# Source lookups of a graph attention layer: one PSUM tile per half chunk becomes one fixed PSUM tile used in two quarters

## The chip, the cores and the metric

The kernel runs on one core of a Trainium2 chip. The metric is device time in microseconds (us). The engines are TensorE (PE in the profile; its weight loads are PEld), VectorE (DVE), ScalarE (ACT), GpSimd (POOL) and SyncE (SP, which here only issues DMAs). An instruction of one engine that needs the result of another waits for a semaphore count, and each engine runs its own list of instructions strictly in order.

## The reference, cut to what matters

There are 6250 nodes with 128 features and 100,000 edges, sorted by destination. Two graph convolutions come first, then an attention layer over the same edges, each followed by a residual sum and a layer norm. The part that matters here is the attention layer:

```python
z = h @ fc_w.T
rh = r_h @ fc_r_w.T
zs = z[src]
zd = z[dst]
e = zs @ aw[0] + zd @ aw[1] + rh @ aw[2]
e = jnp.where(e >= 0, e, NEG_SLOPE * e)
m = jax.ops.segment_max(e, dst, num_segments=N)
ex = jnp.exp(e - m[dst])
alpha = ex / jax.ops.segment_sum(ex, dst, num_segments=N)[dst]
agg = jax.ops.segment_sum(alpha[:, None] * (zs + rh), dst, num_segments=N)
out = jax.nn.relu(agg + z @ loop_w)
```

`zs @ aw[0]` is one number per node, fetched for each edge by the node that the edge starts from. That fetch, 100,000 lookups in a table of 6250 numbers, is what the change is about.

## The kernel before, in words

Edges are cut into 49 chunks of 2048 (`NC`, `CC`), and nodes into 49 blocks of 128 (`NB`). The program has stages one after the other: preparation and sorting, first convolution, second convolution (with the dot products of edge features beside it), and the attention stage, which is the last and holds everything that follows.

In the attention stage two strands run together. The main loop goes over the chunks: `shares` places the attention shares of a chunk (L1254 to L1264), `pick` gathers the rows of source nodes by matmuls with a 0/1 mask and by indirect DMAs (L532, L537, L541), `scatter` sums them by destination (L578), `edge_part` does the same with the edge features (L1280 to L1304), and `Pieces` finishes blocks of nodes as they are complete. The other strand, `scores`, works out the attention shares ahead of the loop, in eight batches of chunks (2, 5, then 7 chunks each): `ends` looks up the destination's number, `starts` the source's, and `softmax` turns a batch into shares. The first main-loop chunk of a batch can't begin before that batch's softmax is done. `scores` is a generator; `deal` takes so many of its steps at fixed points of the main loop, and each `yield` in it ends a step.

`starts(c)` handles a chunk in two halves of 1024 edges, so there are 98 half chunks in all. For each half, a row of source numbers modulo 128 is loaded and broadcast to all partitions (`rk`, L1105), and turned into a 0/1 matrix by VectorE (L1138). VectorE also makes `ohb`, which marks the block of each edge (L1140). TensorE then multiplies, for each of the half's 8 groups of 128 edges, the 0/1 matrix with the table of 49 blocks, three times because the table is split into three bf16 parts (L1145): 24 matmuls into a PSUM tile `k` of 128x392 float32. VectorE multiplies the tile by `ohb` into `sel` (L1148) and sums over the blocks (L1149), which leaves one number per edge in `asr`. The pool `ps_k` has one buffer, one PSUM bank; the pools of the stage take all eight banks. `sel` has one buffer too.

The order in which instructions stand on each engine isn't the program's text order. A scheduler orders them when the program is built, by priorities that follow the text (and the steps of `deal`) and by when it reckons each instruction is ready. The instructions of `starts` are so mixed with those of the main loop. The order is fixed once built, and the semaphore waits are put in then, after a tracking of which instruction touches which tile.

Of the kernel before, what the change touches and what calls it, by code (L numbers as in the profile page):

```python
# [9 lines left out]
F32 = mybir.dt.float32  # L10
# [9 lines left out]
P = 128  # L20
# [7 lines left out]
NL = CC // P  # L28
# [10 lines left out]
def gnn_kernel(ctx, tc, x, src, dst, ea, ew, W1, b1, W2, b2, fcw, fcrw, attn, loopw, out):  # L39
# [11 lines left out]
    nc = tc.nc  # L51
# [3 lines left out]
    NB = -(-N // P)  # L55
# [155 lines left out]
    adp = keep.tile([P, 2, 3, NB + 1], BF16, name="adp")  # L211
# [386 lines left out]
    with tc.tile_pool(name="prep", bufs=1) as prep, tc.tile_pool(name="ps_p", bufs=3, space=PSUM) as ps_mm, \  # L598
# [113 lines left out]
        ps = ps_mm.tile([P, 4, D], F32, name="mm")  # L712
# [134 lines left out]
    def steps_to(c):  # L847

        b = next(b for b, (c0, n) in enumerate(sorts) if c < c0 + n)
        return 2 * sum(sorts[b]) + b + 1  # L850

    with tc.tile_pool(name="xs0", bufs=1) as xp, tc.tile_pool(name="ps_d", bufs=3, space=PSUM) as ps_mm, \
# [8 lines left out]
        with tc.high_priority():  # L861
            for c0 in range(0, NC, 7):
# [4 lines left out]
                for c in range(c0, c0 + n):  # L867
                    m = ms[:, c - c0]
                    ps = ps_w.tile([3, WC], F32, name="win")
# [11 lines left out]
            ps = ps_w.tile([P, NB], F32, name="win")  # L881
# [9 lines left out]
    with tc.tile_pool(name="conv", bufs=2) as wp, tc.tile_pool(name="hp", bufs=2) as hp, \  # L891
# [18 lines left out]
        start, total = done[0], steps_to(NC - 1)  # L910
# [169 lines left out]
    with tc.tile_pool(name="look", bufs=2) as lp, tc.tile_pool(name="conv3", bufs=2) as wp, \  # L1080
# [11 lines left out]
        for j in range(J):  # L1092
            ps = ps_c.tile([P, 3, NB], F32, name="rec")
            nc.tensor.matmul(ps, wide[:, P + j : 2 * P + j], adp[:, 1, :, :NB], start=True, stop=j == 0)
            if j:
                nc.tensor.matmul(ps, wide[:, j : P + j], adp[:, 1, :, 1:], start=False, stop=True)
            nc.scalar.copy(a_d[:, :, j, :], ps)
        rks = {}
        HC = CC // 2

        def sources(i):

            if i < 2 * NC:
                rks[i] = lp.tile([P, HC], BF16, name="rk", bufs=3)
                nc.sync.dma_start(rks[i], srow[i // 2, None, i % 2 * HC : (i % 2 + 1) * HC].to_broadcast([P, HC]))  # L1105
# [26 lines left out]
        def starts(c):  # L1132

            for h in range(2):
                of = slice(h * NL // 2, (h + 1) * NL // 2)
                sources(2 * c + h + 2)
                mk = rks.pop(2 * c + h)
                nc.vector.tensor_scalar(mk, mk, iotap, None, op0=OP.is_equal)  # L1138
                ohb = lp.tile([P, NB, NL // 2], BF16, name="ohb")
                nc.vector.tensor_tensor(ohb, iota_t[:, :NB, : NL // 2], blks[:, c, None, of].to_broadcast([P, NB, NL // 2]),  # L1140
                                        op=OP.is_equal)
                ps = ps_k.tile([P, NL // 2, NB], F32, name="k")
                for s in range(NL // 2):
                    for k in range(3):
                        nc.tensor.matmul(ps[:, s, :], mk[:, s * P : (s + 1) * P], adp[:, 0, k, :NB], start=k == 0, stop=k == 2)  # L1145
                yield
                sel = lp.tile([P, NL // 2, NB], F32, name="sel", bufs=1)
                nc.vector.tensor_mul(sel, ps, ohb.rearrange("p b s -> p s b"))  # L1148
                nc.vector.tensor_reduce(asr[:, 1 + c * NL + of.start : 1 + c * NL + of.stop], sel, AX.X, OP.add)  # L1149

        ready = {}
# [74 lines left out]
        def scores():  # L1226
            for b, (c0, n) in enumerate(batches):

                c0, c1 = c0 + (b > 0), min(c0 + n, NC - 1)
                for c in range(c0, c1 + 1, 4):  # L1230
                    yield from ends(c, min(4, c1 + 1 - c))
                for c in range(c0, c1 + 1):
                    yield from starts(c)
                yield from softmax(b)
                yield
# [73 lines left out]
        for b, (c0, n) in enumerate(batches):  # L1309
# [6 lines left out]
            for c in range(c0, c0 + n):  # L1316
# [16 lines left out]
                ps = edge_part(c, aw, c - c0)  # L1333
# [16 lines left out]
    with tc.tile_pool(name="slow", bufs=1) as sl, tc.tile_pool(name="ps_o", bufs=2, space=PSUM) as ps_mm, \  # L1350
# [4 lines left out]
        for k, cs in enumerate((slice(0, CF), slice(CF, NC))):  # L1355
            some = [P, cs.stop - cs.start, GS]
# [8 lines left out]
        ps = ps_mm.tile([1, P], F32, name="mm")  # L1365
# [67 lines left out]
        with tc.If(slow > 0):  # L1433
# [8 lines left out]
            ps = ps_mm.tile([P, NB], F32, name="mm")  # L1442
# [22 lines left out]
            with tc.For_i(0, E, SG) as e:  # L1465
                d_f, _, _, sc = scores(e, False)
                with tc.For_i(0, NB, 1) as b:
# [4 lines left out]
                    ps = ps_mm.tile([P, SG], F32, name="mm")  # L1472
# [9 lines left out]
            with tc.For_i(0, E, SG) as e:  # L1482
                d_f, zr, er, sc = scores(e, True)
                with tc.For_i(0, NB * P, P) as at:
                    m = sl.tile([SG, P], F32, name="m")
                    nc.vector.tensor_scalar(m, iota[:SG, :P], d_f[:, 0:1], sc[:, 0:1], op0=OP.is_equal, op1=OP.mult)
                    for to, of in ((sum_x, zr), (sum_r, er), (den, ones)):
                        ps = ps_m2.tile([P, P], F32, name="mm2")
# [34 lines left out]
```

## Time and profile before

| what | value |
|---|---|
| time, median of 3 runs | 2011.86 us (1997.91 to 2015.49) |
| the profiled execution's own time | 2359.94 us |
| its span, first to last instruction | 2358.0 us |
| granted TensorE clock, mean | 0.855 |
| attention stage in the profile | about 1440 us to the end, 918 us |
| lookups of sources (L1145) | from 1442.3 to 2092.3 us, 98 half chunks |

The profiled execution takes 348 us more than the median of the runs without a profile, so sums made on it are sums on a slower copy of the same program. Its lines give, for a group of instructions, the busy time in us, the mean duration of one in ns, and the idle time of the engine just before them with what ended that idle time ("<-"). "issue" means that the engine waited for nothing that the profile shows.

### The profile page before, as it was taken

The page shows a single profiled execution, that of the slowest core. Times are in us where ns is not written, and L with a number is a line of the kernel's source. Part 1 is how long each engine was busy: PE and PEld are TensorE (multiplying, and loading weights), DVE is VectorE, ACT ScalarE, POOL GpSimd, SP SyncE. Part 2 cuts the span into 40 slices and gives each one's busy share as a digit, 9 for nine tenths or more (in the row PEclk, how much of TensorE's full clock was granted, in tenths as well). Part 3 has the DMA queues.
Part 4 walks back from the last instruction along what each step waited for, and adds up shares of the span by engine and source line. Part 5 has one row for each costly group of instructions (what it writes and reads, how often), then busy time and mean ns, then how long its engine had stood idle before and what let it go on. Part 6 is the DMA issues. An engine that isn't in the chain of part 4 may idle for free.

```text
span 2358.0 us, 79261 instructions
## 1 busy us (share of the span) xinstructions
PE 1796.2 (76%) x34061; PEld 1573.2 (67%) x34061; DVE 1657.7 (70%) x3281; ACT 952.3 (40%) x3099; POOL 1078.9 (46%) x941
## 2 busy tenths in 40 slices
PE   2767888887878766788887874588876787888884
PEld 2556777777777655677776763577765777777774
DVE  7885767767766445888777875887876787776552
ACT  1254444443534443556565652133323242334332
POOL 4054445454564526677676762133333233424441
PEclk9877888888878788899999995688998898899887
DMA  2123323243231446566656674445554555544441
GB/s 53 32 86 104 101 66 119 58 137 90 81 116 53 144 149 201 178 205 215 207 196 195 212 227 148 123 124 153 138 148 133 145 148 154 145 133 133 132 135 48
DMA packets 257393, 316.38 MB, mean 134 GB/s; under 512 B 38349, under 2 KB 194131, under 8 KB 249466
## 3 DMA queue, kind: packets, MB, share of 16 engines
q1 hardware_dynamic: 224823, 249.62, 33.8%
q0 software_dynamic: 23520, 48.22, 9.4%
q10 hardware_dynamic: 8688, 13.37, 1.7%
q8 instruction: 270, 4.42, 0.8%
q14 instruction: 92, 0.75, 0.1%
HBM read 265.14 MB, written 45.97 MB: 132 GB/s over the span
## 4 chain that ended last, share of the span: by engine, by line
PE 60%; DVE 17%; issue 12%; another core or an unknown queue 4%; ACT 3%; DMA 3%; POOL 0%; DVEq 0%; ACTq 0%; SPq 0%; POOLq 0%
PE win L578 24%; PE g L532 17%; PE r L758 3%; PE r L1293 2%; PE rec L1263 2%; PE k L1145 2%; DVE sel L1148 2%; PE rec L1304 2%; DVE wm L547 2%; PE rec L821 1%; DVE put L814 1%; ACT got L537 1%; DVE ohm L809 1%; PE mm L383 1%
## 5 line engine op out<-in xcount | busy, mean ns | idle before, releaser
L541 POOL DMA_INDIRECT far<-g,sidx x490 | 721.7, 1473 | 509.1 <-PE win L578 350.1
L532 PE MATMUL g<-hot,mask 128*32 128x128 bf16 x21168 | 553.0, 244 | 256.8 <-issue 232.2
L537 ACT ACTIVATE got<-g,swt 128x128 f32<-128x128 f32 x1764 | 489.9, 377 | 597.7 <-PE g L532 242.7
L532 PEld LDWEIGHTS <-mask 128*32 128x32 bf16 x21168 | 409.3, 108 | 369.6 <-issue 349.1
L541 POOL DMA_INDIRECT far<-zd,sidx x245 | 299.9, 1224 | 608.4 <-PE win L578 503.9
L578 PE MATMUL win<-wm,got 128*128 128x144 f32 x3528 | 544.6, 313 | 11.2 <-DVE acc L583 7.1
L578 PEld LDWEIGHTS win<-wm,got 128*128 128x128 f32 x3528 | 505.5, 211 | 32.9 <-issue 18.1
L547 DVE TENSOR_TENSOR wm<-iota,sdst 128x1728 f32<-128x1728 f32 x147 | 286.7, 1950 | 1.1 <-POOL hot L343 0.8
L571 ACT ACTIVATE wm<-wm,swt 128x64 f32<-128x64 f32 (+1 forms) x735 | 201.2, 355 | 77.4 <-DVE wm L554 39.6
L583 DVE TENSOR_TENSOR acc<-acc,win 128x144 f32 x147 | 44.5, 303 | 208.6 <-PE win L578 199.7
L578 PE MATMUL win<-wm,far 128*128 128x64 f32 (+1 forms) x1470 | 186.1, 273 | 6.5 <-DMA far<-g,sidx 6.0
L578 PEld LDWEIGHTS win<-wm,far 128*128 128x128 f32 x1470 | 182.3, 195 | 7.1 <-DMA far<-g,sidx 6.2
L1145 PE MATMUL k<-adp,rk 128*128 128x49 bf16 x2352 | 104.5, 199 | 57.0 <-DVE sel L1148 33.6
L1145 PEld LDWEIGHTS <-rk 128*128 128x128 bf16 x2352 | 92.1, 107 | 73.7 <-issue 47.6
L1030 DVE TENSOR_TENSOR et<-et,ar_row 128x2048 f32<-128x2048 f32 (+1 forms) x49 | 111.6, 2278 | 4.4 <-DMA et<-in_edge_attr_dram 4.4
L1031 DVE TENSOR_REDUCE dots<-et 128x16 f32<-128x2048 f32 (+1 forms) x49 | 112.0, 2286 | 1.7
L1148 DVE TENSOR_TENSOR sel<-k,ohb 128x392 f32<-128x392 f32 x98 | 83.8, 855 | 21.2 <-PE k L1145 10.1
L758 PE MATMUL r<-oh,first 128*128 128x48 bf16 x784 | 80.1, 268 | 9.4 <-DVE oh L754 8.2
L1304 PE MATMUL rec<-pl,sw 128*128 128x144 f32 x196 | 45.1, 363 | 47.9 <-ACT sw L1298 45.2
L1298 ACT COPY sw<-r 128x256 f32<-128x256 f32 (+1 forms) x49 | 18.3, 373 | 156.2 <-PE r L1293 74.9
L809 DVE TENSOR_TENSOR ohm<-iota_t,pm 128x2048 bf16<-128x2048 bf16 x49 | 59.7, 1218 | 30.0 <-PE rec L821 22.7
L758 PEld LDWEIGHTS <-first 128*128 128x128 bf16 x784 | 69.4, 120 | 15.8 <-issue 7.5
(408 smaller groups left out, 2320.5 us busy)
## 6 DMA issues: line engine op xcount, KB each, us to landing
et<-in_edge_attr_dram SPq DMA_DIRECT2D x97, 512.0 KB
et<-in_edge_attr_dram SPq DMA_DIRECT2D x48, 1024.0 KB
mask<-masks SPq DMA_DIRECT2D x98, 384.0 KB
rk<-srow SPq DMA_DIRECT2D x98, 256.0 KB
mask<-srd SPq DMA_DIRECT2D x49, 384.0 KB
masks<-mask SPq DMA_DIRECT2D x49, 384.0 KB
far<-g,sidx POOLq DMA_INDIRECT x490
dr<-dinvd SPq DMA_DIRECT2D x22, 256.0 KB
```

The lines of the kernel that those rows point to most:

```text
L532: nc.tensor.matmul(ps[32 * q : 32 * q + 32, g, :], mask[:, (g0 + g) * P + 32 * q : (g0 + g) * P + 32 * q + 32], hot[:, 4 * (g0 + g) + q, k ...
L537: nc.scalar.activation(got[:, g, :], ps[:, g, :], AF.Copy, scale=swt[:, c, g0 + g : g0 + g + 1])
L541: nc.gpsimd.indirect_dma_start(out=got, out_offset=None, in_=table[:, :], in_offset=bass.IndirectOffsetOnAxis(ap=sidx[:, c, g : g + 1], ax ...
L547: nc.vector.tensor_tensor(wm[:, : GP * WC].rearrange("p (g w) -> p g w", w=WC), iota[:, None, 1 : WC + 1].to_broadcast([P, GP, WC]), sdst[ ...
L571: nc.scalar.activation(m, m, AF.Copy, scale=swt[:, c, g : g + 1])
L578: nc.tensor.matmul(ps[:, n0 : n0 + m.shape[-1]], rows[g], m, start=g == 0, stop=g == G - 1)
L758: nc.tensor.matmul(ps, first, oh[:, :, t], start=t == 0, stop=t == TC - 1)
L1030: nc.vector.tensor_mul(et[:n], et[:n], ar_row[:n, None, :].to_broadcast([n, TC, D]))
L1031: nc.vector.tensor_reduce(dots[:n, c, :], et[:n], AX.X, OP.add)
L1145: nc.tensor.matmul(ps[:, s, :], mk[:, s * P : (s + 1) * P], adp[:, 0, k, :NB], start=k == 0, stop=k == 2)
L1148: nc.vector.tensor_mul(sel, ps, ohb.rearrange("p b s -> p s b"))
L1304: nc.tensor.matmul(ps, sw[:p, g, :], pl[:p, g, :], start=g == 0, stop=g == len(sizes) - 1)
```

## The change

The PSUM tile is allocated once, ahead of the loop, as `two_k`, instead of once per half chunk. The 24 matmuls of a half are split into two runs of 12, each on its own half of the tile's columns (four groups of 128 edges, a quarter of a chunk). After each run of 12, VectorE multiplies that half of the tile into the same half of `sel`: two instructions of 128x196 in the place of one of 128x392. The sum over the blocks (L1149 before, L1153 after) stays one instruction per half chunk. The `yield` stands between the second run of matmuls and its multiply.

```diff
+        two_k = ps_k.tile([P, NL // 2, NB], F32, name="k")
         rks = {}
...
-                ps = ps_k.tile([P, NL // 2, NB], F32, name="k")
-                for s in range(NL // 2):
-                    for k in range(3):
-                        nc.tensor.matmul(ps[:, s, :], mk[:, s * P : (s + 1) * P], adp[:, 0, k, :NB], start=k == 0, stop=k == 2)
-                yield
                 sel = lp.tile([P, NL // 2, NB], F32, name="sel", bufs=1)
-                nc.vector.tensor_mul(sel, ps, ohb.rearrange("p b s -> p s b"))
+                for s0 in range(0, NL // 2, NL // 4):
+
+                    some = slice(s0, s0 + NL // 4)
+                    for s in range(s0, s0 + NL // 4):
+                        for k in range(3):
+                            nc.tensor.matmul(two_k[:, s, :], mk[:, s * P : (s + 1) * P], adp[:, 0, k, :NB], start=k == 0, stop=k == 2)
+                    if s0:
+                        yield
+                    nc.vector.tensor_mul(sel[:, some], two_k[:, some], ohb.rearrange("p b s -> p s b")[:, some])
                 nc.vector.tensor_reduce(asr[:, 1 + c * NL + of.start : 1 + c * NL + of.stop], sel, AX.X, OP.add)
```

## The prediction, made before the changed kernel ran

> **What bounds the kernel now.** I first read the page's busy shares and the two groups that the change touches, to see how large they are at all.
>
> ```profile
> PE 1796.2 (76%) x34061; PEld 1573.2 (67%) x34061; DVE 1657.7 (70%) x3281; ACT 952.3 (40%) x3099; POOL 1078.9 (46%) x941
> ...
> L1145 PE MATMUL k<-adp,rk 128*128 128x49 bf16 x2352 | 104.5, 199 | 57.0 <-DVE sel L1148 33.6
> ...
> L1148 DVE TENSOR_TENSOR sel<-k,ohb 128x392 f32<-128x392 f32 x98 | 83.8, 855 | 21.2 <-PE k L1145 10.1
> ```
>
> No engine is full. The lookups take 104.5 us of TensorE and 83.8 us of VectorE, and at their hand-offs each engine waits for the other: TensorE 33.6 us for the multiply, VectorE 10.1 us for the matmuls. 33.6 us is the most obvious thing the change can win.
>
> The table by stage shows where those 33.6 us can matter. Columns: length, then busy time (and instructions) of PE, PEld, DVE, ACT, POOL, then clock, DMA share and GB/s.
>
> ```profile
> 1440.00:1560.00 120.00, 71.49 (x1352) 62.05 (x1351) 97.42 (x276) 19.62 (x71) 27.23 (x21) 0.61 0.52 139
> ...
> 1800.00:1900.00 100.00, 78.86 (x1614) 69.73 (x1604) 75.98 (x180) 32.10 (x115) 29.46 (x27) 0.90 0.53 144
> ...
> 2100.00:2200.00 100.00, 86.05 (x1673) 76.72 (x1674) 66.92 (x135) 41.52 (x143) 46.41 (x34) 0.90 0.52 142
> ```
>
> The first 120 us of the attention stage are VectorE's (81% busy, TensorE 60%): lookups for the first two batches, before the main loop is in full swing. Then, up to 2095 us, lookups and main loop run mixed, with TensorE and VectorE within 6 us of each other per 100 us. Neither has slack that the other could lean on, so what makes one wait soon makes the other wait. After 2095 us there are no lookups, and the change can do nothing there.
>
> The lookups' own waits, first from 1443 to 1560 us (26 half chunks), then from 1560 us on (72):
>
> ```profile
>   DVE sel L1148: 24.8, 17
>   remote: 4.7, 1
>   PE k L1145: 3.6, 5
> ```
>
> ```profile
>   issue: 13.3, 30
>   DVE sel L1148: 8.8, 12
>   PE k L1145: 6.5, 6
> ```
>
> So 24.8 of the 33.6 us are in the first stretch, in 17 of 26 hand-offs. Later the scheduler puts other matmuls between the lookups, and only 12 of 72 hand-offs are waited for. What one bare hand-off costs is seen in the timeline at 1448 us (start, duration, engine):
>
> ```profile
> 1448.37 1.18 PE L1145 MATMUL k<-adp,rk 128*128 128x49 bf16 x24 [1.17 <-DVE sel L1148]
> ...
> 1449.60 0.85 DVE L1148 TENSOR_TENSOR sel<-k,ohb 128x392 f32<-128x392 f32 x1
> ...
> 1450.50 0.70 PE L1145 MATMUL k<-adp,rk 128*128 128x49 bf16 x13 [0.94 <-DVE sel L1148]
> ```
>
> Matmuls 1.18, about 0.05 to VectorE, multiply 0.85, about 0.05 back: 2.13 us from one half's first matmul to the next half's. TensorE and VectorE never work on the tile together.
>
> **The change, part by part.** *Do the two places take turns?* The point is that TensorE should fill one half of the bank while VectorE reads the other. The built order of the changed kernel says no: each of the 195 later runs of 12 matmuls waits for a VectorE count that includes the multiply of the run just before it, which reads the other half of the bank. Matmuls and multiplies of the lookups stay strictly alternate, with twice as many hand-offs of half the size. A rule of the Trainium skill speaks to this (page "PSUM — Partial Sum Buffer", section "PSUM bank collisions raise a hardware error"): two engines must not touch one bank in the same 32-partition quadrant at once, even in different columns, and software has to guard by bank and quadrant, not by address. Both places use all 128 partitions of one bank, so the wait is not an oversight. The row above shows an engine waiting for its own columns; it can't tell a wait for the bank from a wait for the bytes. By byte-wise waits, the first run of a half would find its columns long free, and up to the 33.6 us would go: 2360 - 34 = 2326. By the rule, nothing overlaps, and the sum is the one below. I take the rule, because the built waits agree with it.
>
> *Two multiplies for one.* 98 instructions of 392 columns become 196 of 196. No row has that size; the nearest reads from PSUM are these (1560 to 2095 us):
>
> ```profile
> L1148 DVE TENSOR_TENSOR sel<-k,ohb 128x392 f32<-128x392 f32 x72 | 62.0, 861 | 12.6 <-PE k L1145 6.5 <-remote 2.1 <-PE win L578 1.7
> ...
> L583 DVE TENSOR_TENSOR acc<-acc,win 128x144 f32 x29 | 8.7, 301 | 4.6 <-PE win L578 3.4 <-issue 1.1
> ...
> L1123 DVE TENSOR_TENSOR got<-rec,oh 128x72 f32<-128x72 f32 (+2 forms) x10 | 2.2, 217 | 5.8 <-remote 5.4 <-PE rec L1117 0.4
> ```
>
> From 72 to 144 columns is 84 ns, 1.17 ns a column, which leaves some 0.13 us that doesn't depend on size. Then 196 columns take 0.13 + 0.73/2 = 0.49 us, and the pair 0.13 us more than the one before: 98 x 0.13 = 12.9 us of VectorE. From the other side, if all of the time scaled with columns, nothing would be added. I take 0.13, since two rows of small size show it.
>
> *Twice the hand-offs, bare.* A run of 12 matmuls shows as 0.66 us (at 1711 us), not 0.59, since the start isn't halved. A half chunk becomes 2 x (0.66 + 0.05 + 0.49 + 0.05) = 2.50 us instead of 2.13: 0.37 us more. In the first stretch all 26 halves at that price give 9.6 us (the longer multiply is in it). The least is nothing, if other work covers the second hand-off.
>
> *Twice the hand-offs, mixed with the main loop.* What is queued behind a run of 12 that waits are the matmuls of L532, L578 and L1293 behind it on TensorE, and through them ACT's copies and the sums on VectorE (L583), which already wait. In the built orders, weighed by durations of these rows, 11 of 97 hand-offs before have no other matmul in between and 10 more have under 0.5 us; after, it is 25 and 28 of 195. So the cover per hand-off is no better, and there are twice as many. At the present price each, 8.8 us on 72, the 72 new ones add 8.8 us. Bounds: nothing if all are covered; 72 x 0.59 = 42 us if none is. Below nothing isn't excluded: shorter blocks on TensorE could let other work start earlier. I take 8.8, the row of the same wait.
>
> *VectorE's growth in that stretch* is 72 x 0.13 = 9.4 us, counted in full, because VectorE and TensorE alternate as each other's cause of waiting there. With cover it would be nothing.
>
> *Moved.* The first multiply now stands ahead of the `yield`, and the scheduler fits the rest anew. In the built order the first batch's softmax has its last product (L1216) after 10 half chunks of lookups instead of 14, so the main loop may start some lookups sooner; but lookups not done before it must be done beside it, since the counts meet again at chunk 10 (44 halves in both). I cost it at nothing: work of the loop hides it, and without that cover it is at most the 4 halves at 2.5 us, 10 us either way. On SP's queue the `rk`, `mask` and `et` loads shift by a few places; POOL's order is unchanged; on ACT the copy L1298 stands later in some early chunks. No DMA is added.
>
> Sum: 9.6 + 8.8 + 9.4 = 27.8 us, so the profiled execution would go from 2360 to 2388 us. Waits on semaphores and VectorE durations are in the runs without a profile as well, so I put the same 28 us on the median: 2012 + 28 = **2040 us**, 1.4% slower. About 1% is what a measurement of this kernel can tell from no change.
>
> **The rivals.** *The finer grain wins (not slower).* The mechanism is not overlap in the bank, but that a 0.66 us run fits into gaps of TensorE's order where a 1.18 us block did not. In its favour: 33.6 us of TensorE waits, 24.8 of them in a stretch where TensorE is only 60% busy; and the earlier first softmax. Price: the wait of the first stretch goes, 24.8 us, and VectorE's 12.9 us are hidden in its idle time: 2012 - 25 = 1987. It decides if the new order leaves less than about half of the present wait per hand-off. Against it: 53 of 195 hand-offs have little or no cover, and VectorE at 81% in the first stretch is what TensorE waits for. Chance 0.23.
>
> *All is covered.* The scheduler hides the hand-offs, and only part of VectorE's growth is seen, at half of 12.9: 2012 + 6 = 2018. For it: the 60 hand-offs of 72 that are not waited for today. Against: two engines at 76% and 79% in step. Chance 0.15.
>
> *The forecast's own case*, slower by over 1%: chance 0.62. Its range is 2025 (half of the sum) to 2073 (the upper bound, 9.6 + 42 + 9.4 = 61).
>
> **How the numbers follow.** The time is the likeliest case's, 2040. The range goes from 1985, where the finer grain has won all the first stretch's wait, to 2073, the bound of uncovered hand-offs; it leaves out the case in which later waits go as well, and disturbed orders beyond the bound. Chances: faster by over 1% 0.23, within 0.15, slower 0.62.
>
> **What would show it.** In the changed profile: 196 multiplies at about 490 ns (at 430 the growth is nil; above 550 it is larger); TensorE's wait for the multiply in some 40 to 60 places and above 40 us in all, where the finer grain would show it well below 33.6; from 1443 to 1560 us as many lookups in more time; the last lookup at about 2120 us instead of 2092; and 263 us from there to the end, as before. A matmul of the lookups that runs while a multiply of them runs would show that the turns do take place. The prediction is wrong if the new order shortens other waits in the mixed stretch, above all L1304's for ACT (38.5 us there), which no cost above includes.

## The result, and the profile after

| | before | changed |
|---|---|---|
| time, median of 20 runs each | 2006.49 us (1990.97 to 2024.70) | 2024.86 us (2008.15 to 2036.26) |
| ratio | | 1.0095, 95% interval 1.0072 to 1.0119 |

The changed kernel is slower by 0.95%, 18.4 us. One thing has to be known to read the profiles: the same program takes about 2006 us in some sets of runs and about 2405 us in others, and the profile of before (2359.94 us) is of the second kind and the changed kernel's (2008.15 us) of the first, so the 348 us between profile and median weren't the price of profiling. Every ratio below is taken within its own set of runs. In place of the kernel before, the profile of a kernel that takes the same time as it (ratio 0.9992, below: quarters in chunks 0 to 12 only, half chunks in one piece after that) serves for the mixed stretch, the part of the attention stage in which lookups and main loop run beside each other.

The page of the changed kernel, engines and the two groups of the change:

```profile
PE 1610.8 (80%) x34061; PEld 1468.7 (73%) x34061; DVE 1660.9 (83%) x3379; ACT 943.9 (47%) x3099; POOL 1065.5 (53%) x941
...
L1149 PE MATMUL k<-adp,rk 128*128 128x49 bf16 x2352 | 103.0, 192 | 61.9 <-DVE sel L1152 57.6
...
L1152 DVE TENSOR_TENSOR sel<-k,ohb 128x196 f32<-128x196 f32 x196 | 96.9, 495 | 11.4 <-PE k L1149 10.6
```

The multiply of 196 columns takes 495 ns. TensorE waits for it 84 times, for 57.6 us in all; before, in the profile of 2360 us, it was 29 times and 33.6 us, on 98 hand-offs. A hand-off is one exchange between the two engines: TensorE fills, VectorE reads, TensorE may fill again. That the places don't take turns is seen in the timeline (start, duration, engine):

```profile
1301.00 0.66 PE L1149 MATMUL k<-adp,rk 128*128 128x49 bf16 x12 [1.76 <-DVE sel L1152]
1301.14 1.94 DVE L547 TENSOR_TENSOR wm<-iota,sdst 128x1728 f32<-128x1728 f32 x1
1303.01 0.48 DVE L1152 TENSOR_TENSOR sel<-k,ohb 128x196 f32<-128x196 f32 x1
1303.54 0.66 PE L1149 MATMUL k<-adp,rk 128*128 128x49 bf16 x12 [1.89 <-DVE sel L1152]
```

A run of 12 ends at 1301.66. Its multiply is behind 1.94 us of other work on VectorE, and ends at 1303.49; 0.05 us later the next run starts, into the other half of the bank, after 1.89 us of waiting. In the whole trace no lookup matmul runs while a lookup multiply runs. So a hand-off costs not only the multiply's own 0.49 us, but also what stands ahead of the multiply on VectorE.

The mixed stretch, from 117 us after the first lookup to the last lookup, first in the changed kernel, then in the one that has half chunks there (length, then busy time of PE, PEld, DVE, ACT, POOL, clock, DMA share, GB/s):

```profile
1352.30:1795.30 443.00, 379.47 (x8653) 343.88 (x8642) 406.54 (x1026) 167.23 (x575) 174.22 (x146) 0.97 0.63 173
```

```profile
1362.10:1787.80 425.70, 360.60 (x8527) 331.97 (x8527) 397.87 (x950) 166.78 (x574) 174.86 (x143) 0.97 0.65 178
```

17.3 us more, in which VectorE is 8.7 us more busy (406.54 - 397.87) and 8.6 us more idle (36.5 against 27.8). From the last lookup to the end it is 210.9 us against 215.3, so a little is made up. These are one execution each, and the changed kernel's is the fastest of its 20 runs: it comes to its first lookup 9.8 us sooner (1235.3 against 1245.1), by work that the change doesn't touch, so that the two spans differ by only 3.1 us. The lookups' waits in this stretch, the changed kernel first:

```profile
  DVE sel L1152: 25.9, 49
  PE k L1149: 7.0, 10
...
  DVE rk L1139: 0.8, 2
```

```profile
  DVE sel L1153: 14.6, 19
  DVE rk L1139: 8.4, 12
  PE k L1150: 2.1, 3
```

TensorE's wait for the multiply goes up by 11.3 us and VectorE's for the matmuls by 4.9 us. TensorE's wait for the 0/1 matrix (`rk`) all but goes, and its wait for a tile of the main loop (`put`) falls too, by 10.2 us:

```profile
PE rec L1267 <- DVE put L1263: 4.5, 7, 1.3
```

```profile
PE rec L1268 <- DVE put L1264: 14.7, 16, 1.6
```

So the new wait takes the place of old ones, and TensorE's idle time as a whole doesn't rise: 63.5 us (443.00 - 379.47) against 65.1 (425.70 - 360.60). What rises on TensorE is its busy time, by 18.9 us, and not in the lookups alone. The gather's matmuls (L532), which the change doesn't touch, in the same two stretches (length, busy time of PE and PEld):

```profile
1352.30:1795.30 443.00, 94.07 (x4216) 68.19 (x4204) 0.97 0.63 173
```

```profile
1362.10:1787.80 425.70, 80.64 (x4107) 62.33 (x4107) 0.97 0.65 178
```

13.4 us more for 109 more matmuls, at the same granted clock; 109 at the mean of the second line would be 2 us. Followed in order of time, TensorE goes over from one line's matmuls to another line's 591 times in the changed kernel's stretch and 447 times in the other's: the lookups' shorter runs cut the main loop's runs up as well. A run of 24 that is cut in two shows as 0.14 us more (2 x 0.66 - 1.18), so 144 more changes are, as an estimate, 20 us. That fits the 18.9 us; that it is the cause is not shown, and the ends of matmuls are modelled in this profile.

### The profile page after: what moved, and what is told of

Read it like the earlier page. It is cut to its first block, busy times and chain, and to the rows that moved or that the text cites. A ratio compares the mean times of both kernels' runs of the same rounds, so it can differ in the third digit from the quotient of the medians.

```text
span 2006.2 us, 79392 instructions
## 1 busy us (share of the span) xinstructions
PE 1610.8 (80%) x34061; PEld 1468.7 (73%) x34061; DVE 1660.9 (83%) x3379; ACT 943.9 (47%) x3099; POOL 1065.5 (53%) x941
## 4 chain that ended last, share of the span: by engine, by line
PE 43%; DVE 31%; DMA 12%; issue 7%; ACT 4%; POOL 1%; DVEq 0%; SPq 0%; ACTq 0%; POOLq 0%
PE win L578 18%; PE g L532 8%; DVE wm L547 4%; DMA rk<-srow 3%; PE r L758 3%; DVE sel L1152 2%; DMA far<-g,sidx 2%; PE r L1297 2%; DVE put L814 2%; PE rec L1267 2%; DMA mask<-srd 2%; PE rec L821 2%; ACT got L537 2%; DVE et L1030 2%; DVE ohm L809 2%
## 5 line engine op out<-in xcount | busy, mean ns | idle before, releaser
L541 POOL DMA_INDIRECT far<-g,sidx x490 | 698.1, 1425 | 324.5 <-PE win L578 165.6
L541 POOL DMA_INDIRECT far<-zd,sidx x245 | 311.0, 1269 | 455.6 <-PE win L578 351.0
L578 PE MATMUL win<-wm,got 128*128 128x144 f32 x3528 | 526.5, 305 | 19.3 <-issue 11.2
L578 PEld LDWEIGHTS win<-wm,got 128*128 128x128 f32 x3528 | 484.7, 203 | 37.7 <-issue 19.1
L532 PE MATMUL g<-hot,mask 128*32 128x128 bf16 x21168 | 405.2, 229 | 94.8 <-issue 68.0
L532 PEld LDWEIGHTS <-mask 128*32 128x32 bf16 x21168 | 336.7, 101 | 132.2 <-issue 106.2
L578 PE MATMUL win<-wm,far 128*128 128x64 f32 (+1 forms) x1470 | 188.0, 273 | 11.8 <-DMA far<-g,sidx 11.5
L578 PEld LDWEIGHTS win<-wm,far 128*128 128x128 f32 x1470 | 182.6, 195 | 12.9 <-issue 12.8
L1149 PE MATMUL k<-adp,rk 128*128 128x49 bf16 x2352 | 103.0, 192 | 61.9 <-DVE sel L1152 57.6
L1149 PEld LDWEIGHTS <-rk 128*128 128x128 bf16 x2352 | 93.7, 102 | 80.4 <-issue 67.9
L1152 DVE TENSOR_TENSOR sel<-k,ohb 128x196 f32<-128x196 f32 x196 | 96.9, 495 | 11.4 <-PE k L1149 10.6
L821 PE MATMUL rec<-put,ohm 128*128 128x90 bf16 x784 | 59.8, 246 | 22.8 <-DVE put L817 22.3
L814 DVE TENSOR_TENSOR put<-ohg,rec 128x1360 bf16<-128x1360 bf16 x49 | 76.8, 1567 | 0.0
L821 PEld LDWEIGHTS <-ohm 128*128 128x128 bf16 x784 | 56.5, 165 | 27.6 <-DVE put L817 18.1
```

The costliest lines, as they stand in the source:

```text
L532: nc.tensor.matmul(ps[32 * q : 32 * q + 32, g, :], mask[:, (g0 + g) * P + 32 * q : (g0 + g) * P + 32 * q + 32], hot[:, 4 * (g0 + g) + q, k ...
L541: nc.gpsimd.indirect_dma_start(out=got, out_offset=None, in_=table[:, :], in_offset=bass.IndirectOffsetOnAxis(ap=sidx[:, c, g : g + 1], ax ...
L578: nc.tensor.matmul(ps[:, n0 : n0 + m.shape[-1]], rows[g], m, start=g == 0, stop=g == G - 1)
L814: nc.vector.tensor_tensor(put[:, :, : G * F].rearrange("p t (g f) -> p t g f", f=F), ohg[:, :, :, None].to_broadcast([P, TC, G, F]), rec[: ...
L821: nc.tensor.matmul(ps, ohm[:, :, t], put[:, t, :], start=t == 0, stop=t == TC - 1)
L1149: nc.tensor.matmul(two_k[:, s, :], mk[:, s * P : (s + 1) * P], adp[:, 0, k, :NB], start=k == 0, stop=k == 2)
```

## The experiments

Two theories were set against each other. *Hand-offs*: the cost is the second strict exchange between TensorE and VectorE per half chunk, with the waits and the shorter runs that it brings. *VectorE's work*: the cost is the longer sum of multiplies (by rows 96.9 us against 83.8), on an engine that is 92% busy in the mixed stretch. A third possibility stood beside both: that the scheduler, given other instructions, happened on a worse order.

**Two multiplies, one hand-off.**

```diff
-                nc.vector.tensor_mul(sel, ps, ohb.rearrange("p b s -> p s b"))
+                for s0 in range(0, NL // 2, NL // 4):
+                    some = slice(s0, s0 + NL // 4)
+                    nc.vector.tensor_mul(sel[:, some], ps[:, some], ohb.rearrange("p b s -> p s b")[:, some])
```

> The kernel before with one edit: all 24 matmuls of a half chunk as before, then two multiplies of 196 columns in the place of one of 392. VectorE's growth (96.9 - 83.8 = 13.1 us by the two profiles) without a second hand-off. If VectorE's work sets the added time, this alone costs 10 to 14 us (ratio 1.005 to 1.007). If the second hand-off is the cost, it costs nothing (within 3 us). By the prediction's sum, where growth is 12.9 of 27.8 us, scaled to the 18.4 us measured, it costs 8 to 9 us.

Measured: 1993.24 against 2005.76 us, ratio 0.9951 (0.9927 to 0.9974). All of VectorE's growth is there, and the kernel is 10 us faster by the ratio (12.5 by the medians), not slower. So VectorE's work isn't the cost, against both the second theory and the prediction's share. The changed kernel differs from this one by the second hand-off and the order that comes of it, the earlier first multiply among it, and lies 1.4% above it (1.0095 against 0.9951 of the same kernel before). The timeline of this kernel also shows why the growth is smaller than the rows say:

```profile
1504.03 0.89 DVE L1150 TENSOR_TENSOR sel<-k,ohb 128x196 f32<-128x196 f32 x2
1504.84 0.48 DVE L554 TENSOR_TENSOR wm<-fiota,sdst 128x320 f32<-128x320 bf16 x1
```

Two multiplies of some 0.49 us take 0.89 us together, and the next instruction starts 0.08 us before they end: VectorE instructions that follow each other without a wait overlap by about 0.1 us, so that the fixed part of 0.13 us is mostly hidden. Start to start, two multiplies take 0.81 us here (1504.03 to 1504.84), and one of 392 columns took 0.75 us in the kernel with half chunks:

```profile
1501.99 0.83 DVE L1153 TENSOR_TENSOR sel<-k,ohb 128x392 f32<-128x392 f32 x1
1502.74 1.21 DVE L1259 TENSOR_TENSOR ohm<-iota_t,pm 128x2048 bf16<-128x2048 bf16 x1
```

That is 0.06 us a half chunk, 6 us in all, not 12.9. Over all multiplies of these two traces whose successor starts before they end, the means are 0.83 us for two and 0.78 us for one, which says the same. Where the 10 us gain of this kernel comes from is taken up with the last two experiments.

**The dose: eighths of a chunk.** In the changed kernel, `NL // 4` becomes `NL // 8` in the loop, and the step ends ahead of the last multiply:

```diff
-                for s0 in range(0, NL // 2, NL // 4):
+                for s0 in range(0, NL // 2, NL // 8):
...
-                    if s0:
+                    if s0 == NL // 2 - NL // 8:
                         yield
```

> The changed kernel with its pieces halved once more: four runs of 6 matmuls and four multiplies of 98 columns per half chunk, on the same bank. A dose: three extra multiplies and three extra hand-offs per half in the place of one. If VectorE's work alone sets the time, 98 x 3 x 0.134 = 39 us over the kernel before (ratio 1.020). If growth and hand-offs both count as in the changed kernel, 3 x 18.4 = 55 us (1.027). If the change's cost is an accident of its order, anything below 25 us.

Measured: 2143.60 us, ratio 1.0713 (1.0660 to 1.0766), 138 us slower, more than any of the expectations. The two groups, by line:

```profile
L1149 PE MATMUL k<-adp,rk 128*128 128x49 bf16 x2352 | 140.2, 197 | 109.3 <-DVE sel L1152 103.9 <-issue 1.9 <-DVE adp L269 1.3
L1152 DVE TENSOR_TENSOR sel<-k,ohb 128x98 f32<-128x98 f32 x392 | 125.2, 319 | 50.0 <-PE k L1149 48.2
```

VectorE's whole busy time is 1687.9 us, 27 us above the changed kernel's, so growth of its work can't make 138 us. TensorE's wait for the multiply is 103.9 us and VectorE's for the matmuls 48.2, and TensorE's busy time is 1689.2 us, 78 us above the changed kernel's. The mixed stretch has a lower granted clock, 0.86 (the last figure but two) where the changed kernel has 0.97:

```profile
1349.30:1921.60 572.30, 463.52 (x9077) 403.82 (x9076) 452.94 (x1222) 171.98 (x586) 183.54 (x155) 0.86 0.53 144
```

Matmuls that the edit doesn't touch take longer too (L578 of the attention stage, 334 ns each against 301). From one extra hand-off to three the added time goes from 18 to 138 us, far more than threefold. But the dose isn't a clean one: how much of the 138 us is waiting, how much shorter runs and how much the lower clock, and which of them brings the others, isn't shown.

**Quarters in one part of the stage only.**

```diff
-                for s0 in range(0, NL // 2, NL // 4):
+                step = NL // 4 if c < 13 else NL // 2
+                for s0 in range(0, NL // 2, step):
...
-                    if s0:
+                    if s0 + step == NL // 2:
                         yield
```

> The changed kernel, with quarters for the chunks 0 to 12 only (26 half chunks, those of the first stretch), and half chunks in one run of 24 matmuls and one multiply for the rest. The prediction's sum put 9.6 of 27.8 us there, a third: of the 18.4 us measured 6 us. If VectorE's growth alone counts, 26 x 0.134 = 3.5 us. If the first stretch is hidden, as its many waits before the first chunk of the main loop might be, nothing.

> The counterpart: quarters for the chunks 13 to 48 only (72 half chunks), half chunks in one piece in the first stretch. The prediction's sum put 18.2 of 27.8 us there: of the 18.4 us measured 12 us. If VectorE's growth alone counts, 72 x 0.134 = 9.6 us. If the mixed stretch covers the hand-offs and the growth, nothing.

Measured: quarters in chunks 0 to 12 only, 2005.13 us, ratio 0.9992 (0.9958 to 1.0025); in chunks 13 to 48 only (`c >= 13`), 2020.32 us, ratio 1.0075 (1.0053 to 1.0097), 15 us. The cost lies in the mixed stretch. The first stretch shows none, to within some 7 us.

The traces show how that comes about. Half chunks done (the sums over blocks, in brackets) at two times after the first lookup, first in the changed kernel, then in the one with half chunks in the first stretch:

```profile
1235.30:1339.70 104.40, 12.17 (x22) 0.60 0.54 149
1235.30:1456.20 220.90, 24.30 (x44) 0.81 0.58 161
```

```profile
1248.20:1352.60 104.40, 14.27 (x26) 0.60 0.60 157
1248.20:1469.40 221.20, 24.22 (x44) 0.79 0.60 161
```

With quarters 22 are done in 104.4 us and with half chunks 26, and the 26th comes 13.5 us later, at 117.8 us. But with quarters the main loop begins after 13 half chunks instead of 16 (49.1 against 52.9 us after the first lookup), and at 221 us both have 44 done and begin chunk 10 of the main loop (the second line of each fence). The slower start is made up, in one execution of each.

**Two places in two banks.** The gather's pool gives up one of its three banks; the control gives it up too, and leaves it unused.

```diff
-            tc.tile_pool(name="ps_g3", bufs=3, space=PSUM) as ps_g
+            tc.tile_pool(name="ps_g3", bufs=2, space=PSUM) as ps_g
...
-        two_k = ps_k.tile([P, NL // 2, NB], F32, name="k")
+        two_k = [ps_k.tile([P, NL // 4, NB], F32, name="k%d" % i, bufs=1) for i in range(2)]
...
-                            nc.tensor.matmul(two_k[:, s, :], mk[:, s * P : (s + 1) * P], adp[:, 0, k, :NB], start=k == 0, stop=k == 2)
+                            nc.tensor.matmul(two_k[s0 * 4 // NL][:, s - s0, :], mk[:, s * P : (s + 1) * P], adp[:, 0, k, :NB], start=k == 0, stop=k == 2)
...
-                    nc.vector.tensor_mul(sel[:, some], two_k[:, some], ohb.rearrange("p b s -> p s b")[:, some])
+                    nc.vector.tensor_mul(sel[:, some], two_k[s0 * 4 // NL], ohb.rearrange("p b s -> p s b")[:, some])
```

> The changed kernel with its two places in two banks (a tile of 128x196 each, used in turn), paid for with one of the three buffers of the gather's PSUM pool. Same multiplies, same runs of 12 matmuls. To be read against e7. If the strict alternation in one bank is the cost, this is 18 to 30 us faster than e7, and TensorE's wait for the multiply falls below 20 us. If the cost is the number of pieces or the scheduler's order, the two are within 5 us.

> The control for e6: the changed kernel as it is, with two buffers in the place of three for the gather's PSUM pool, the freed bank unused. A gather of a chunk needs three such tiles. If the third buffer is of use, this is 5 to 30 us slower than the changed kernel; else it equals it at about 2025 us.

In this set the kernel before takes 2405.14 us. Measured: two banks 2421.49 us, ratio 1.0057 (1.0022 to 1.0092); one bank, with the gather's bank unused, 2447.84 us, ratio 1.0176 (1.0138 to 1.0215). The second bank is worth 26 us. The lookups' waits, in one bank first and then in two (the lines between are other waits):

```profile
  DVE sel L1152: 54.8, 57
...
  PE k L1149: 22.7, 30
```

```profile
  PE k L1149: 29.8, 17
...
  DVE rk L1139: 21.9, 19
...
  DVE sel L1152: 14.3, 14
```

TensorE's wait for the multiply falls from 54.8 to 14.3 us. And here the turns do take place:

```profile
1496.21 1.18 PE L1149 MATMUL k<-adp,rk 128*128 128x49 bf16 x24 [1.07 <-DVE rk L1139]
1497.20 0.49 DVE L1152 TENSOR_TENSOR sel<-k,ohb 128x196 f32<-128x196 f32 x1
```

The 24 matmuls run through until 1497.39, and the multiply of the first 12 starts at 1497.20, while they run. In the whole trace 61 of the 196 multiplies overlap with lookup matmuls, and none of those in one bank. With as many pieces and multiplies as in one bank, the alternation is what is taken away; the scheduler's order changes with it, as with every edit here. Two banks are also two tiles: a wait put in for the bank isn't told apart from one put in for the tile. But the two banks don't pay for the gather's bank: the two-bank kernel still takes 0.57% more than the kernel before. What the third gather buffer is worth alone wasn't measured, since the changed kernel itself was not in this set.

**The kernel before, again.**

> The kernel before unchanged, for a second profile, since the first one's execution took 348 us more than the median. If the second takes about 2005 us, its waits can be set beside those of the changed kernel: the hand-off account says that TensorE's wait for the multiply is clearly below the 57.6 us (84 times) of the changed kernel, and VectorE's wait for the lookups below 10.6 us; the account by VectorE's work says that VectorE is about 13 us less busy in the attention stage and waits as much.

> The kernel before unchanged, once more for a profile, to be set beside the changed kernel's if this set of runs takes about 2005 us. By the hand-off account TensorE waits for the multiply some 30 times for about 30 us (84 times and 57.6 us in the changed kernel); by the account of VectorE's work, the two profiles differ in VectorE's busy time in the attention stage and not in its idle time.

The two took 2401.87 and 2441.44 us, so they can't be set beside the profile of the changed kernel (2008.15 us), and that comparison stays undone. They serve for the two-bank pair, the first of them from the same set: TensorE waited for the multiply 29 times for 33.6 us and 30 times for 32.1 us, against 57 times and 54.8 us with quarters in one bank.

**The block marks laid out as they are read.**

```diff
-                ohb = lp.tile([P, NB, NL // 2], BF16, name="ohb")
-                nc.vector.tensor_tensor(ohb, iota_t[:, :NB, : NL // 2], blks[:, c, None, of].to_broadcast([P, NB, NL // 2]),
-                                        op=OP.is_equal)
+                ohb = lp.tile([P, NL // 2, NB], BF16, name="ohb")
+                nc.vector.tensor_tensor(ohb, iotab[:, None, :NB].to_broadcast([P, NL // 2, NB]),
+                                        blks[:, c, of, None].to_broadcast([P, NL // 2, NB]), op=OP.is_equal)
...
-                nc.vector.tensor_mul(sel, ps, ohb.rearrange("p b s -> p s b"))
+                nc.vector.tensor_mul(sel, ps, ohb)
```

> The kernel before with the block marks laid out as the multiply reads them (groups outer, blocks inner, next to each other) in the place of reading every eighth element; one multiply, one hand-off as before. If the stride is why a column costs 1.85 ns in this multiply and 1.17 in the sum of 144 columns, the multiply falls from 0.855 to about 0.59 us, and making the marks rises by 0.0 to 0.2 us. If VectorE's work in the lookups sets the time, 98 x 0.1 to 0.25 us less is 10 to 25 us faster (ratio 0.988 to 0.995). If only hand-offs and order matter, within 5 us.

Measured: 2384.93 against 2405.14 us, ratio 0.9896 (0.9854 to 0.9938): faster than the kernel before and, by the two ratios, than the changed one. By line:

```profile
L1148 DVE TENSOR_TENSOR sel<-k,ohb 128x392 f32<-128x392 f32 x98 | 54.6, 557 | 28.1 <-PE k L1145 15.9 <-remote 11.7
L1140 DVE TENSOR_TENSOR ohb<-iotab,blks 128x392 bf16<-128x392 bf16 x98 | 54.3, 554 | 0.0
```

The marks in a profile of the kernel before from the same set:

```profile
L1140 DVE TENSOR_TENSOR ohb<-iota_t,blks 128x392 bf16<-128x392 bf16 x98 | 34.4, 351 | 0.0
```

From that profile to this one the multiply goes from 853 to 557 ns and making the marks from 351 to 554 ns, 0.09 us less per half chunk, some 9 us in all. The gain is twice that. This fits the view that it isn't only the work that counts but also where it stands: the multiply is inside the hand-off, and 0.30 us shorter; the marks are made ahead of it. TensorE's wait for the multiply falls from 33.6 to 19.9 us, in 20 places. An order that happens to suit would fit as well.

**Both faster edits together, a later end of the step, an uneven split.** The first joins the layout above with two multiplies after all 24 matmuls:

> Both edits that were faster: block marks with the blocks inner, and two multiplies after all 24 matmuls (one hand-off per half chunk). If the gain of each is less VectorE work on the way of the hand-off or a finer grain, they add: ratio 0.983 to 0.990. If the gain of the two multiplies was only the order that the scheduler happened to find, it is 0.985 to 1.00 with no rule.

The second moves the `yield` of the kernel before:

```diff
-                yield
                 sel = lp.tile([P, NL // 2, NB], F32, name="sel", bufs=1)
                 nc.vector.tensor_mul(sel, ps, ohb.rearrange("p b s -> p s b"))
+                yield
```

> The kernel before with the end of the step moved from ahead of the multiply to behind it, ahead of the sum over blocks: the same instructions, in another order by the scheduler. The change moves its first multiply so. If moving it is free, as the prediction costed it, within 5 us of the kernel before. If the order alone moves the time as much as the changes tried here, 10 us or more either way, and then the 12.5 us by which two multiplies after one run were faster can't be put down to the multiplies.

The third splits the multiply into seven groups and one:

```diff
-                nc.vector.tensor_mul(sel, ps, ohb.rearrange("p b s -> p s b"))
+                for some in (slice(0, NL // 2 - 1), slice(NL // 2 - 1, NL // 2)):
+                    nc.vector.tensor_mul(sel[:, some], ps[:, some], ohb.rearrange("p b s -> p s b")[:, some])
```

> The kernel before with the multiply split unevenly after all 24 matmuls: seven groups (343 columns) and one group (49). It has the extra instruction and the fixed cost of two equal multiplies, not their shorter length. If two equal multiplies were faster since VectorE's blocks are shorter, this is not faster than the kernel before, and up to 13 us slower. If any second instruction leads the scheduler to a better order, it is faster by about as much, 8 to 16 us.

Measured, against 2410.66 us of the kernel before in this set: both edits 2409.92 us, ratio 0.9983 (0.9960 to 1.0005); later end of the step 2408.63 us, 0.9978 (0.9955 to 1.0001); uneven split 2405.81 us, 0.9989 (0.9966 to 1.0013). None can be told from no change. Moving the end of a step cost nothing, as costed, though the interval leaves room for 11 us of gain. A second multiply instruction cost nothing either, in the uneven split. But the two gains don't add: with the better layout and two equal multiplies together, neither gain is seen. So "two shorter multiplies are faster" is no rule, and neither is the better layout's gain of 1%; by what the first experiment's 10 us came about stays open. Its own profile shows VectorE waiting for the lookups' matmuls 0.2 us in all, against 10.6 us in the changed kernel, which fits an order that happens to suit; that this is the cause was not shown. Neither that kernel nor the one with the better layout alone was run in this set, where each might have stood otherwise.

## Why the prediction was right, and where it was not

The forecast was 28 us slower (2012 to 2040); measured were 18.4 us. The direction, the strict alternation as the mechanism and the stretch where most of it lies were right. How the alternation costs time was right only in part, and that the sum for the mixed stretch held is partly luck. By the prediction's own steps:

- *"Do the two places take turns?"* They don't: in the changed kernel the next run starts 0.05 us after the multiply of the other half, and with two banks, which the Trainium skill calls free of collisions (page "PSUM — Partial Sum Buffer", section "PSUM bank collisions raise a hardware error"), they do, and 26 us come back. Taking the rule's side against the reading by bytes gave the right sign; that the wait is there for the bank, and not for the tile, is not shown.
- *"Two multiplies for one"*: 0.49 us was forecast, 495 ns measured. The row was right and the term was not: 12.9 us of VectorE shrink to about 6, since instructions that follow without a wait overlap by about 0.1 us. The fixed part was read from durations; it should have been read from start to start. One of the two rows was also misread: the 217 ns of L1123 are a mean over three shapes, and its five instructions of 72 columns take 226 ns, which by the same sum makes 0.50 us and 0.15 us more per pair.
- *"Twice the hand-offs, bare"*, 9.6 us in the first stretch: this step failed. Quarters there alone cost -1.6 us (interval -8.4 to +5.0). The lookups themselves do come later, by more than forecast (the 26th by 13.5 us), but the cost isn't on the path that sets the time: the main loop begins with three fewer of them done, and the counts meet again at chunk 10 with 44 done, as *"Moved"* had said. The step that failed is counting the slower lookups in full.
- *"Twice the hand-offs, mixed with the main loop"*, 8.8 us, and *"VectorE's growth in that stretch"*, 9.4 us: together 18.2 us; measured were 15 us with quarters there alone, and 17.3 us between the two profiles' stretches. The sum held. How it is shared out did not: growth alone cost nothing in the first experiment, so, as far as that experiment's own gain isn't an accident of order, nearly all of it belongs to the second hand-off, for which 8.8 us were put. And it isn't simply a wait: TensorE waits 11.3 us more for the multiply, near the 8.8, but 17.8 us less for `rk` and `put`, and is 18.9 us more busy, in shorter runs. For that the sum has no term in this stretch; the start of a run that "isn't halved" was counted in the first stretch alone. VectorE's added busy time, 8.7 us, looks like the growth term, but isn't a cost that the two multiplies bring without the second hand-off. So two terms that failed in part add up to about the measured time.
- *"Moved"*, costed at nothing: the kernel with the end of the step moved is within its interval of no change. That test moves it in the kernel before, not in the changed one.
- *The rival "the finer grain wins"* fell by its own test: it asked for TensorE's wait to stay well below 33.6 us, and it is 57.6. *"All is covered"* is nearer than its chance of 0.15 made it: the 1.0095 lies just inside 1%, and the first stretch was in fact covered. The forecast of over 1% failed by the 9.6 us of that stretch.
- *What would show it*: above 40 us of TensorE waits was right (57.6); 40 to 60 places was low (84). No lookup matmul ran during a lookup multiply, as forecast. The times of day (last lookup at 2120 us) can't be judged, since the profile of before is of an execution of 2360 us. Nor can the sign of being wrong, TensorE's wait for ACT at L1304: the 38.5 us belong to that execution, and in the stretch it is 2.0 us in the changed kernel against 3.7 us in the one with half chunks there.

## What to carry to other kernels

Cutting a PSUM tile into two places of one bank bought no overlap here; it doubled the strict exchanges between TensorE and its reader. Two tiles in two banks did overlap. Count such exchanges, and what stands ahead of the reader on its own engine, before counting the work: here the added work alone cost nothing, and the second exchange per tile 1.0 to 1.4%, against the kernel before and against the one with two multiplies and one exchange. Look at the busy time as well as at the waits: an exchange that cuts up an engine's runs can show as busier matmuls, with no more idle time. And a cost counts only where the work is on the path: the first lookups came later by 13.5 us, and the end did not, to within some 7 us. Gains of 0.5 and 1% from one small edit each were not seen when the two were joined, so such a gain is no rule yet.

## What was not expected of the hardware

- TensorE stood still with no cause that the profile shows: ahead of the gather's matmuls (L532) "issue" is 232 to 274 us in the three profiles of the kernel before, and 68 us in that of the changed kernel, with a granted clock of 0.83 to 0.855 against 0.90. It may be a difference between chips: where the record names the chip, the sets of about 2405 us ran on two, and the one of about 2006 us on a third. One set on each doesn't show it. A profile must be matched to its runs by its time before it is compared.
- VectorE instructions that follow each other without a wait overlap: two multiplies of 495 ns each take 0.89 us, and the next starts 0.08 us before they end.
- A multiply of 392 columns takes 855 ns when its bf16 operand is read in steps of 16 bytes, and 557 ns when its elements lie next to each other. The Trainium skill has a mechanism for it (page "SBUF — State Buffer", section "Door 1: The DMA port swizzle"): accesses that each go to a new line of 16 bytes pay. The two rows are in line with that. The same place gives 8 bf16 elements as how far one can stride for free; the step here is 8, and it wasn't free. No run tries another step, so the mechanism isn't shown.
